# Transposed aggregations of two graphs: one 128-row matmul, or two of 64 rows into two PSUM banks

## The chip, the cores and the metric

The kernel runs on one core of a Trainium2 chip, in fp32 throughout. The metric is the device time of one execution in microseconds; before the change the median of three runs is 2634.96 us (2633.36 to 2637.23).

## The reference, cut to what matters

There are 128 graphs of 64 nodes, each node with 512 features, an adjacency matrix per graph, and four graph layers in a row. Each is followed by a residual and a layer norm: `x = layernorm(x + layer(x, adj))`. With the parts that don't matter here left out:

```python
# layer 0: attention from scores s = x @ w @ a
A = exp(leaky(8 * tanh((s_i + s_j) / 8))) * adj;  A = A / sum(A) * sum(adj)
out = A @ x @ w
# layer 1: A = adj * exp(q k^T), normalized;  out = A @ v
# layer 2: a weight per node (softmax over the graph) times x @ Wv
# layer 3: two hypergraph convolutions, G being 64 x 64 for each graph
h = layernorm(relu(G @ (x @ W1.T) + b1))          # 1024 features
out = G @ (h @ W2.T) + b2
```

In layers 0 and 3 the kernel aggregates first and multiplies by the weights after: it needs (A x)^T, (G x)^T and (G h)^T, with the features on the partitions, as the stationary operand of the product that follows.

## The kernel before, in words

Two graphs of 64 nodes make a tile of 128 rows, and two tiles (`GT = 2`) make a group, so there are 32 groups. The function `run(g)` is one group's whole way through the four layers. It is a Python generator with a `yield` between its stages; up to four groups are in flight, a new one is started every four steps, and at each step each running group emits its next stage, the newest group first. The tile framework's scheduler then orders the instructions on each engine, moves some of them past others, and puts in the semaphores. So the order within a stage of the code is not always the order on the engine, and pieces of several groups stand next to each other on TensorE.

The aggregation with transposition is `gathered(xt, bd)` (L282). For each tile `t` it takes one buffer `tr` of the pool `ps_tr` (two buffers, one PSUM bank each: 4 chunks x 128 columns of fp32), and for each of the four chunks of 128 features runs one matmul (L288):

```python
nc.tensor.matmul(tr[:, c, :], xt[:, t, ts(c, P)], bd[:, t, :], start=True, stop=True)
```

The stationary operand is the tile's x, 128 rows by 128 features. The moving operand is `bd`, a block-diagonal matrix of 128 x 128: it holds the 64 x 64 matrices of the tile's two graphs, with zeros outside the two blocks. After each tile ScalarE copies the bank to SBUF (L289). `gathered` is called in layer 0 with `e_bd` (result used by L296 with `w0_sb`) and in layer 3 with `g_bd` (used by L296 with `w3a_sb`). The second aggregation of layer 3, of `h` with its eight chunks, is written out in `run` at L502 and copied at L503 into one tile `ghT` per `t`; it feeds L296 with `w3b_sb`.

Around these on TensorE stand: `transposed` (L278), which uses the same pool `ps_tr` and is emitted twice per step, for two different groups; `product_T` (L305) and `product` (L296); `scores` (L320), which for each chunk issues two matmuls of 128 rows with 64 stationary and 64 moving columns, one per graph, into different halves of the PSUM partitions; L374, matmuls of the same kind for the layer-0 scores; `row_sums` (L327), which multiplies a block-diagonal matrix by one column of ones; L419, L440 and L458 of layers 1 to 3.

Of the other engines: VectorE does the residuals and layer norms (L346 is the last step of a norm), ScalarE the copies out of PSUM and the exponentials (L447 are those of layer 2, which wait for the maximum `mx` of VectorE), GpSimd the power for the norm and some additions, and SyncE the loads and stores.

Of the kernel before, what the change touches and what calls it, by code (L numbers as in the profile page):

```python
# [10 lines left out]
FP = mybir.dt.float32  # L11
# [4 lines left out]
P = 128  # L16
B, N, D, DH = 128, 64, 512, 1024
T = B * N // P
GT = 2
# [3 lines left out]
KC = D // P  # L23
KH = DH // P
# [7 lines left out]
def kernel(  # L32
# [23 lines left out]
    nc = tc.nc  # L56
    cpool = ctx.enter_context(tc.tile_pool(name="const", bufs=1))
    xpool = ctx.enter_context(tc.tile_pool(name="xpool", bufs=IN_FLIGHT + 1))
    chunks = ctx.enter_context(tc.tile_pool(name="chunks", bufs=3))
    scratch = ctx.enter_context(tc.tile_pool(name="scratch", bufs=1))  # L60
    stage = ctx.enter_context(tc.tile_pool(name="stage", bufs=2))
    work = ctx.enter_context(tc.tile_pool(name="work", bufs=3))
    small = ctx.enter_context(tc.tile_pool(name="small", bufs=2 * IN_FLIGHT))
    ps_mm = ctx.enter_context(tc.tile_pool(name="ps_mm", bufs=4, space=bass.MemoryType.PSUM))
    ps_tr = ctx.enter_context(tc.tile_pool(name="ps_tr", bufs=2, space=bass.MemoryType.PSUM))
# [9 lines left out]
    halves = ((slice(0, N), slice(0, N)), (slice(N, P), slice(N, P)))  # L75
# [50 lines left out]
    def weights(w, rows, cols, name, pool=None):  # L126
        t_ = (pool or cpool).tile([P, rows // P, cols], FP, name=name)
        nc.gpsimd.dma_start(out=t_, in_=w.rearrange("(c p) o -> p c o", p=P))
        return t_
# [22 lines left out]
    w3b_sb = weights(w3b, DH, D, "w3b_sb")  # L152
# [120 lines left out]
    def transposed(xt):  # L273
        xT = work.tile([P, KC, GT * P], FP, name="xT")
        for t in range(GT):
            tr = ps_tr.tile([P, KC, P], FP, name="tr")
            for c in range(KC):
                nc.tensor.transpose(tr[:, c, :], xt[:, t, ts(c, P)], ident)  # L278
            nc.scalar.copy(xT[:, :, ts(t, P)], tr)
        return xT  # L280

    def gathered(xt, bd):  # L282

        gT = work.tile([P, KC, GT * P], FP, name="xT")
        for t in range(GT):
            tr = ps_tr.tile([P, KC, P], FP, name="tr")
            for c in range(KC):
                nc.tensor.matmul(tr[:, c, :], xt[:, t, ts(c, P)], bd[:, t, :], start=True, stop=True)  # L288
            nc.scalar.copy(gT[:, :, ts(t, P)], tr)  # L289
        return gT  # L290

    def product(lhsT, t, w, cols=slice(0, D), chunks=KC):

        ps = ps_mm.tile([P, D], FP, name="mm")
        for k in range(chunks):
            nc.tensor.matmul(ps, lhsT[:, k, ts(t, P)], w[:, k, cols], start=(k == 0), stop=(k == chunks - 1))  # L296
        return ps
# [40 lines left out]
    def layer_norm(xt):  # L338
        st = small.tile([P, GT, 6], FP, name="st")
        mv = small.tile([P, GT, 2], FP, name="mv")  # L340
        for t in range(GT):
            nc.vector.bn_stats(st[:, t, :], xt[:, t, :])  # L342
            nc.vector.bn_aggr(mv[:, t, :], st[:, t, :])
        rstd = rstd_of(mv)
        for t in range(GT):
            nc.vector.tensor_scalar(xt[:, t, :], xt[:, t, :], mv[:, t, 0:1], rstd[:, t : t + 1],  # L346
                                    ALU.subtract, ALU.mult)
# [6 lines left out]
    def on_diagonal(dst, e, adj):  # L354

        for rows, cols in halves:
            nc.vector.tensor_mul(dst[rows, :, cols], e[rows], adj[rows])
        return dst


    def run(g):
        xt = xs.pop(g)
# [9 lines left out]
        for t in range(GT):  # L372
            for rows, cols in halves:
                nc.tensor.matmul(ps[rows, t, :N], s[:, t : t + 1].to_broadcast([P, N]), ident[:, cols],  # L374
                                 start=True, stop=True)
# [4 lines left out]
        nc.scalar.activation(e, e, AF.Exp, scale=8.0)  # L380
        bd = on_diagonal(next_e(), e, adj)
        yield
        gT = gathered(xt, bd)
        f = small.tile([P, GT], FP, name="f")
        nc.vector.reciprocal(f, row_sums(bd))  # L385
        nc.vector.tensor_mul(f, f, radj)
# [8 lines left out]
        xT = transposed(xt)  # L395
# [17 lines left out]
        bd = on_diagonal(next_e(), e, adj)  # L413
# [15 lines left out]
        xT = transposed(xt)  # L429
# [29 lines left out]
        gm = next_g()  # L459
# [7 lines left out]
        yield  # L467


        gT = gathered(xt, gm)  # L470

        for t in range(GT):
            c = work.tile([P, D], FP, name="junk")
# [5 lines left out]
        h = stage.tile([P, GT, DH], FP, name="h")  # L479
# [13 lines left out]
            nc.scalar.activation(h[:, t, :], h[:, t, :], AF.Identity, bias=nm[:, t : t + 1],  # L493
                                 scale=rstd[:, t : t + 1])
        yield
        ghT = []
        for t in range(GT):
            ghT.append(work.tile([P, KH, P], FP, name="ghT"))
            for i in range(KH // KC):
                tr = ps_tr.tile([P, KC, P], FP, name="tr")  # L500
                for c in range(KC):
                    nc.tensor.matmul(tr[:, c, :], h[:, t, ts(i * KC + c, P)], gm[:, t, :], start=True, stop=True)  # L502
                nc.scalar.copy(ghT[t][:, ts(i, KC), :], tr)  # L503
        yield
        for t in range(GT):
            nc.vector.tensor_add(xt[:, t, :], product(ghT[t], 0, w3b_sb, chunks=KH), xt[:, t, :])  # L506
        layer_norm(xt)
        nc.sync.dma_start(out=out_g[g], in_=xt)

# [5 lines left out]
    while g < NG or running:  # L515
        if g < NG and len(running) < IN_FLIGHT and step % APART == 0:
            running.append(run(g))
            g += 1
            if g < NG:
                load(g)  # L520
            if g % GC == 1 and g // GC + 1 < T // CT:
                load_adj(g // GC + 1)
            if g % GC == 2 and g // GC + 1 < T // CT:
                prepare_chunk(g // GC + 1)
        for r in reversed(list(running)):
            if next(r, running) is running:
                running.remove(r)
        if step == 2:
            prepare_1()
        if step == 4:  # L530
            prepare_2()
        if step == 7:
            prepare_3()
        step += 1
# [41 lines left out]
```

## Time and profile before

| | |
|---|---|
| median of 3 runs | 2634.96 us |
| profiled execution, its own time | 2635.76 us |
| its span, first to last instruction | 2634.0 us |
| TensorE busy | 2556.3 us, 97% of the span |
| VectorE busy | 1138.0 us, 43% |
| ScalarE busy | 590.6 us, 22% |
| GpSimd busy | 546.8 us, 21% |
| mean granted TensorE clock | 0.998 |
| instruction pairs (load, multiply) on TensorE | 11272 |

In the profile PE is TensorE's multiplication and PEld its loading of the stationary operand, which overlaps with it; DVE is VectorE, ACT ScalarE, POOL GpSimd, SP SyncE. A line such as `L288 PE MATMUL tr<-g_bd,x 128*128 128x128 f32 x512` names the source line, the engine, the operation, what it writes and reads by the program's names, the stationary operand's size, that of the moving one and the number of instructions. Busy time counts overlapping instructions of an engine once; the mean of one counts the whole length of each, so for matmuls, which are pipelined, busy time divided by the count is nearer to the pace.

One matmul of the program in fp32 appears as two instruction pairs; a transpose (L278) appears as one.

### The profile page before, as it was taken

To read this page: it belongs to the slowest core of one execution; us is meant where nothing else is said; L and a number is where in the kernel's file an instruction comes from. 1 tells how busy PE (TensorE), PEld (TensorE's weight loads), DVE (VectorE), ACT (ScalarE), POOL (GpSimd) and SP (SyncE) were. 2 spreads that over 40 slices of the span, in tenths; PEclk is the share of its full clock that TensorE was granted. 3 is DMA by queue.
4 is the path that set the end of the run, shared out by engine and by line. 5 is a ranking of instruction groups with operands and counts; after the bars stand their busy time and mean duration, and the time that the engine had idled before them with its cause. 6 is when DMAs were issued, how large, how long until landed. Compare 5 with 4: busy or idle time off the path is not lost.

```text
span 2634.0 us, 27593 instructions
## 1 busy us (share of the span) xinstructions
PE 2556.3 (97%) x11272; PEld 1544.1 (59%) x11272; DVE 1138.0 (43%) x2552; ACT 590.6 (22%) x1164; POOL 546.8 (21%) x560
## 2 busy tenths in 40 slices
PE   6999999999999999999999999999999999999998
PEld 4565565655565655565655565655665655665654
DVE  3535453445433455433545434445443445433443
ACT  0222221222221222221122221222221222221221
POOL 4211221212211222211312212212212212211211
PEclk9999999999999999999999999999999999999999
DMA  5000000000000000000000000000000000000000
GB/s 217 32 1 17 5 17 17 16 17 13 8 16 17 21 17 8 10 17 20 17 16 4 14 21 17 17 17 1 17 16 17 17 17 0 17 16 8 9 9 16
DMA packets 22190, 50.31 MB, mean 19 GB/s; under 512 B 1504, under 2 KB 1504, under 8 KB 22064
## 3 DMA queue, kind: packets, MB, share of 16 engines
q1 hardware_dynamic: 18560, 35.66, 4.0%
q0 software_dynamic: 3504, 12.89, 1.3%
q8 instruction: 89, 1.46, 0.2%
q14 instruction: 37, 0.30, 0.0%
HBM read 31.76 MB, written 16.78 MB: 18 GB/s over the span
## 4 chain that ended last, share of the span: by engine, by line
PE 87%; DVE 5%; issue 5%; POOL 3%; DMA 0%; ACT 0%; POOLq 0%; DVEq 0%
PE mm L296 57%; PE mm L305 17%; PE tr L288 4%; PE sm L320 2%; POOL rstd L335 2%; DVE x L346 2%; PE tr L278 1%; DVE x L420 1%; PE mm L169 1%; PE mm L225 1%; DVE x L389 1%; PE mm L419 1%; PE sm L327 1%; PE sm L374 0%; DMA junk<-in_a_dram 0%
## 5 line engine op out<-in xcount | busy, mean ns | idle before, releaser
L296 PE MATMUL mm<-wv_sb,xT 128*128 128x512 f32 x1024 | 460.6, 593 | 0.0
L305 PE MATMUL mm<-xT,m_sb 128*128 128x256 f32 x2048 | 458.3, 381 | 2.1 <-DVE hw L254 1.5
L296 PE MATMUL mm<-w3a_sb,xT 128*128 128x512 f32 x1024 | 448.0, 595 | 0.0
L296 PE MATMUL mm<-w3b_sb,ghT 128*128 128x512 f32 x1024 | 444.7, 592 | 0.0
L305 PEld LDWEIGHTS mm<-xT,m_sb 128*128 128x128 f32 x2048 | 385.7, 190 | 70.8 <-issue 17.9
L335 POOL TENSOR_TENSOR rstd<-ve,mhalf 128x2 f32<-128x2 f32 x160 | 127.7, 798 | 1369.9 <-DVE ve L333 1291.0
L296 PEld LDWEIGHTS mm<-w3b_sb,ghT 128*128 128x128 f32 x1024 | 194.5, 190 | 244.4 <-issue 244.4
L296 PEld LDWEIGHTS mm<-w3a_sb,xT 128*128 128x128 f32 x1024 | 191.9, 190 | 231.7 <-issue 229.6
L296 PEld LDWEIGHTS mm<-wv_sb,xT 128*128 128x128 f32 x1024 | 187.2, 190 | 185.8 <-issue 183.9
L385 DVE RECIPROCAL f<-sm 128x2 f32<-128x2 f32 x32 | 5.5, 171 | 617.9 <-PE sm L327 617.9
L296 PE MATMUL mm<-w_sb,xT 128*128 128x512 f32 x512 | 225.2, 593 | 0.4 <-issue 0.4
L346 DVE TENSOR_SCALAR x<-x,mv,rstd 128x512 f32<-128x512 f32 x256 | 185.3, 765 | 75.2 <-POOL rstd L335 75.2
L342 DVE BATCH_NORM_STATS2 st<-x 128x6 f32<-128x512 f32 x256 | 176.0, 688 | 4.7
L485 DVE TENSOR_TENSOR h<-mm,b3a_b 128x512 f32<-128x512 f32 x128 | 88.5, 692 | 193.4 <-PE mm L296 193.4
L296 PEld LDWEIGHTS mm<-w_sb,xT 128*128 128x128 f32 x512 | 97.0, 190 | 122.3 <-issue 122.2
L486 ACT ACTIVATE h<-h 128x512 f32<-128x512 f32 x128 | 80.6, 630 | 387.7 <-DVE h L485 387.7
L506 DVE TENSOR_TENSOR x<-mm,x 128x512 f32<-128x512 f32 x64 | 44.3, 691 | 277.0 <-PE mm L296 277.0
L476 POOL TENSOR_SCALAR x<-x 128x512 f32<-128x512 f32 x64 | 39.7, 620 | 559.9 <-PE tr L288 559.9
L502 PE MATMUL tr<-g_bd,h 128*128 128x128 f32 x1024 | 125.7, 282 | 5.5 <-ACT h L493 5.5
L487 DVE BATCH_NORM_STATS2 st<-h 128x6 f32<-128x512 f32 x128 | 88.8, 694 | 88.4 <-ACT h L486 88.4
L309 ACT ACTIVATE z<-mm,r_c 128x256 f32<-128x256 f32 x128 | 60.6, 473 | 293.7 <-PE mm L305 293.7
L502 PEld LDWEIGHTS tr<-g_bd,h 128*128 128x128 f32 x1024 | 121.3, 195 | 7.7 <-ACT h L493 7.4
(138 smaller groups left out, 2374.4 us busy)
## 6 DMA issues: line engine op xcount, KB each, us to landing
x<-in_x_dram SPq DMA_DIRECT2D x32, 512.0 KB, 3.7
out_dram<-x SPq DMA_DIRECT2D x32, 512.0 KB, 2.8
adj<-in_adjT_dram SPq DMA_DIRECT2D x8, 256.0 KB, 2.8
wv_sb<-in_wv_dram POOLq DMA_DIRECT2D x2, 1024.0 KB, 15.3
w3a_sb<-in_w3a_dram POOLq DMA_DIRECT2D x1, 2048.0 KB, 17.4
w3b_sb<-in_w3b_dram POOLq DMA_DIRECT2D x1, 2048.0 KB, 16.4
h<-in_wqk_dram POOLq DMA_DIRECT2D x2, 1024.0 KB, 5.7
w_sb<-in_w_dram POOLq DMA_DIRECT2D x1, 1024.0 KB, 10.7
```

What stands on the lines that cost most here:

```text
L288: nc.tensor.matmul(tr[:, c, :], xt[:, t, ts(c, P)], bd[:, t, :], start=True, stop=True)
L296: nc.tensor.matmul(ps, lhsT[:, k, ts(t, P)], w[:, k, cols], start=(k == 0), stop=(k == chunks - 1))
L305: nc.tensor.matmul(pz[:, : GT * P], w[:, k, ts(c, P)], xT[:, k, :], start=(k == 0), stop=(k == KC - 1))
L309: nc.scalar.activation(zT[:, c, :], pz[:, : GT * P], AF.Identity, bias=bias[:, c : c + 1])
L320: nc.tensor.matmul(ps[rows, t, :N], zT[:, k, tok], xT[:, k, tok], start=(k == 0), stop=(k == KC - 1))
L335: nc.gpsimd.tensor_tensor(rstd, ve, mhalf, ALU.pow)
L342: nc.vector.bn_stats(st[:, t, :], xt[:, t, :])
L346: nc.vector.tensor_scalar(xt[:, t, :], xt[:, t, :], mv[:, t, 0:1], rstd[:, t : t + 1], ALU.subtract, ALU.mult)
L485: nc.vector.tensor_add(hi, product(gT, t, w3a_sb, ts(i, D)), b3a_b[:, ts(i, D)])
L486: nc.scalar.activation(hi, hi, AF.Relu)
L487: nc.vector.bn_stats(st[:, t, i, :], hi)
L502: nc.tensor.matmul(tr[:, c, :], h[:, t, ts(i * KC + c, P)], gm[:, t, :], start=True, stop=True)
```

## The change

`gathered` now takes both tiles of a group at once and runs, for each chunk and tile, one matmul per graph. `halves` is the pair of slices (0 to 63, 0 to 63) and (64 to 127, 64 to 127): the stationary operand is the 64 rows of one graph by 128 features, the moving operand that graph's own 64 x 64 block of `bd`. The matmuls of the first graphs of the two tiles go into one `tr` buffer, those of the second graphs into the other, and they alternate. When both buffers are full, two ScalarE copies of 128 x 512 (8 runs of 64 columns each) sort them into the destination. The written-out loop for `ghT` is replaced by two calls of `gathered`, of four chunks each, and `ghT` becomes one tile for both `t`, in one buffer where there were three of half the size. The zeros of `bd` outside its blocks are no longer read here, but are still read by `row_sums` and L419.

```diff
-    def gathered(xt, bd):
-        gT = work.tile([P, KC, GT * P], FP, name="xT")
-        for t in range(GT):
-            tr = ps_tr.tile([P, KC, P], FP, name="tr")
-            for c in range(KC):
-                nc.tensor.matmul(tr[:, c, :], xt[:, t, ts(c, P)], bd[:, t, :], start=True, stop=True)
-            nc.scalar.copy(gT[:, :, ts(t, P)], tr)
-        return gT
+    def gathered(dst, src, chunks, bd):
+        trs = [ps_tr.tile([P, KC, GT, N], FP, name="tr") for _ in halves]
+        for c in range(KC):
+            for t in range(GT):
+                for tr, (rows, cols) in zip(trs, halves):
+                    nc.tensor.matmul(tr[:, c, t, :], src[rows, t, ts(chunks + c, P)], bd[rows, t, cols],
+                                     start=True, stop=True)
+        for h, tr in enumerate(trs):
+            nc.scalar.copy(dst.rearrange("p c (t h n) -> p h c t n", h=2, n=N)[:, h], tr)
+        return dst
...
-        ghT = []
-        for t in range(GT):
-            ghT.append(work.tile([P, KH, P], FP, name="ghT"))
-            for i in range(KH // KC):
-                tr = ps_tr.tile([P, KC, P], FP, name="tr")
-                for c in range(KC):
-                    nc.tensor.matmul(tr[:, c, :], h[:, t, ts(i * KC + c, P)], gm[:, t, :], start=True, stop=True)
-                nc.scalar.copy(ghT[t][:, ts(i, KC), :], tr)
+        ghT = work.tile([P, KH, GT * P], FP, name="ghT", bufs=1)
+        for i in range(KH // KC):
+            gathered(ghT[:, ts(i, KC), :], h, i * KC, gm)
         yield
         for t in range(GT):
-            nc.vector.tensor_add(xt[:, t, :], product(ghT[t], 0, w3b_sb, chunks=KH), xt[:, t, :])
+            nc.vector.tensor_add(xt[:, t, :], product(ghT, t, w3b_sb, chunks=KH), xt[:, t, :])
```

The other two calls become `gathered(work.tile([P, KC, GT * P], FP, name="xT"), xt, 0, bd)` in layer 0 and the same with `gm` in layer 3. In the changed file the matmul stands at L289 and the copy at L292, and the lines after them are moved by three (`product` is at L299, `scores` at L323, `row_sums` at L330).

More of the change, by code (lines that the diff above doesn't have):

```diff
@@ L382, in run @@
         yield
-        gT = gathered(xt, bd)
+        gT = gathered(work.tile([P, KC, GT * P], FP, name="xT"), xt, 0, bd)
         f = small.tile([P, GT], FP, name="f")
@@ L467, in run @@
         yield
-        gT = gathered(xt, gm)
+        gT = gathered(work.tile([P, KC, GT * P], FP, name="xT"), xt, 0, gm)
         for t in range(GT):
```

## The prediction

> **What bounds the kernel now.** I read the share of each engine first, then the chain that ended last, then TensorE's waits, then the groups of instructions with shapes kept apart, then TensorE's timeline over half a period. Page parts 1 and 4:
>
> ```profile
> PE 2556.3 (97%) x11272; PEld 1544.1 (59%) x11272; DVE 1138.0 (43%) x2552; ACT 590.6 (22%) x1164; POOL 546.8 (21%) x560
> ...
> PE 87%; DVE 5%; issue 5%; POOL 3%; DMA 0%; ACT 0%; POOLq 0%; DVEq 0%
> ```
>
> TensorE sets the time; no other engine is near half. Its waits, longest first:
>
> ```profile
> PE tr L278 <- DVE x L346: 41.6, 32, 2.5
> PE mm L179 <- DVE junk L352: 16.0, 1, 16.0
> ```
>
> One wait recurs, once in each of the 32 groups: 1.3 us at the second pair of transposes, for the normalized x. The groups the change touches and their neighbours (busy us, mean ns of one):
>
> ```profile
> L502 PE MATMUL tr<-g_bd,h 128*128 128x128 f32 x1024 | 125.7, 282 | 5.5 <-ACT h L493 5.5
> L502 PEld LDWEIGHTS tr<-g_bd,h 128*128 128x128 f32 x1024 | 121.3, 195 | 7.7 <-ACT h L493 7.4 <-issue 0.2
> L288 PE MATMUL tr<-e_bd,x 128*128 128x128 f32 x512 | 65.9, 283 | 2.1 <-issue 2.1
> L288 PE MATMUL tr<-g_bd,x 128*128 128x128 f32 x512 | 63.3, 275 | 0.0
> L320 PEld LDWEIGHTS sm<-xT,z 128*64 128x64 f32 x1024 | 32.4, 138 | 0.6
> L327 PE MATMUL sm<-ones,e_bd 128*128 128x1 f32 x256 | 32.5, 231 | 0.0
> L458 PE MATMUL sm<-bhd,h_bd 128*128 128x64 f32 x128 | 17.8, 262 | 0.0
> ```
>
> One fp32 matmul of the program is two instruction pairs here, load and multiply. The aggregations take 65.9 + 63.3 + 125.7 = 254.9 us, 9.7% of the span, at 0.124 to 0.129 us a pair. The reader is to see that L458, which streams 64 columns, costs 17.8 / 128 = 0.139 and L327, which streams one, 32.5 / 256 = 0.127: **below 128 streamed columns the time of a pair does not fall**. The loads lie end to end (121.3 of 125.7 us at L502). TensorE's timeline (start, length, count):
>
> ```profile
> 1033.60 13.90 PE L296 MATMUL mm<-w3b_sb,ghT 128*128 128x512 f32 x32
> 1047.43 0.45 PE L374 MATMUL sm<-ident,s 128*64 128x64 f32 x8
> 1047.81 7.17 PE L305 MATMUL mm<-xT,m_sb 128*128 128x256 f32 x32
> 1054.82 7.03 PE L296 MATMUL mm<-wv_sb,xT 128*128 128x512 f32 x16
> 1061.68 7.07 PE L305 MATMUL mm<-xT,m_sb 128*128 128x256 f32 x32
> 1068.59 1.95 PE L288 MATMUL tr<-g_bd,x 128*128 128x128 f32 x16
> 1070.38 2.00 PE L288 MATMUL tr<-e_bd,x 128*128 128x128 f32 x16
> 1072.21 0.50 PE L327 MATMUL sm<-ones,e_bd 128*128 128x1 f32 x4
> 1072.64 1.15 PE L320 MATMUL sm<-xT,z 128*64 128x64 f32 x32
> 1073.62 1.10 PE L320 MATMUL sm<-z,xT 128*64 128x64 f32 x32
> ```
>
> From start to start, L288 takes (1070.38 - 1068.59) / 16 = 0.112 us a pair. L320, whose two graphs write different halves of the columns, takes (1073.62 - 1072.64) / 32 = 0.031 us, though its 64-column load lasts 138 ns: two parts of the array work side by side.
>
> [...] 192 ns against 138 for 64 columns fewer is 54 ns, and 0.112 us is such a load. That halving the rows saves nothing no run here shows yet. [...] row tiles (64 x 128) do not occur before. [...] L296 before it runs 0.431 a pair, so it would have handed over at 1033.60 + 32 x 0.431 = 47.38, not 47.43; L374's four side-by-side steps of 0.058 (0.98 us over L320's 16 steps, less entry) are 0.23, not 0.38; the L305 block after it takes 7.01 us against 6.91 for the same block at 1061.68. In and out: 0.05 + 0.15 + 0.10 = **0.30 us**. [...]
>
> **The change part by part**, for one of 32 groups; the order is that which the scheduler gives the changed program.
>
> 1. *Streaming.* Per chunk and tile, two pairs of 128 rows become four of 64 rows with half the columns. Each still loads 128 columns, 0.112 us. If the two row tiles run side by side: 2 x 0.112, as before, so **zero** on 32 matmuls. Bounds: a load of half the rows at half the time would save 16 x 0.056 = 0.9 us in each of four blocks; loads taking turns would cost 16 x 0.112 = 1.8. I take zero, by L320's side-by-side loads.
> 2. *Mode changes.* Four new row-tile blocks: the g aggregation after L288's place, the e aggregation, two for ghT, none next to each other. I take 0.35 each, L374's 0.30 and 0.05 for a first load of 128 instead of 64 columns (54 ns); half to double as bounds. g's block is split in two in 6 groups: 0.35 x 38 / 32 = 0.42. The e block now stands in the middle of L320's first block (7 matmuls before, 9 behind), and a way out and in of that mode was there already: 0.30. ghT: 0.70. Sum **1.4 us**.
> 3. *Order within e.* In 29 groups the e block starts with four matmuls of one bank, then four of the other: the second bank is not yet copied out. Four steps of 2 x 0.112 have no partner: **+0.9**, bounds 0 (a tile overlapping its own two passes) and 0.9. The second ghT block starts two and two: +0.2.
> 4. *Waits for the banks.* Both buffers of tr are now filled by one call and freed by its two ScalarE copies (588 ns each, unchanged in size). The copy starts 0.33 us after the last multiply starts (1069.68 for the eighth L288 at 1068.59 + 7 x 0.112), so the banks are free at 0.9 and 1.5. Between g and e lie four L327 pairs, 14 L320 pairs and mode changes, 0.45 + 0.43 + 0.3 = 1.2; between the ghT calls one L296 matmul, 0.86 and a mode change, 1.15; the second bank is first touched 0.45 (ghT) or 0.9 (e) later. **Zero**, up to 0.5 each if a copy is late. ScalarE now has L447's exponentials between the two ghT pairs; they wait for VectorE's mx, and before, they ran from 1023.9; the second ghT block ends about 1024.3, so they are done in time.
> 5. *The wait of L278.* Before the second x's transposes the changed order has three single L296 matmuls and all four other tr blocks, where there was one. From the start of ghT: 0.35 + 1.8 + 0.86 + 0.35 + 2.0 + 0.86 + 0.9 + 0.86 = 8.0 us, against 7.5 before with a wait of 1.9 in it:
>
> ```profile
> 1019.08 3.84 PE L502 MATMUL tr<-g_bd,h 128*128 128x128 f32 x32
> ...
> 1026.57 0.63 PE L278 MATMUL tr<-ident,x 128*128 128x128 f32 x4 [1.92 <-DVE x L346]
> ```
>
> VectorE's queue keeps its order, so x is there, in this group by 0.5 us and by more in those with shorter waits: **-1.3**; the L296 matmuls are only moved. What is late next: nothing on TensorE in this stretch.
> 6. *Other queues.* SP's DMAs, POOL's and VectorE's work are the same and in the same order; the L320 scores finish about 3 us later, but their result is wanted at L419, 24 us on. ghT in one buffer is rewritten 79 us later, 50 after its last read. Zero; without that cover a delay of 3 us in the scores would reach TensorE. The last group has no L296 to lie under its banks: +2 us once.
>
> Sum per group: 1.4 + 1.1 - 1.3 = +1.2; 32 x 1.2 + 2 = **+41 us** on the profiled execution's 2635.8 (span 2634.0 and 1.8 around it), 2677. The median of the runs lies 0.8 below that execution: **2676**.
>
> **The rivals.**
> *A, the case above*: side by side, 128-column loads set the pace. Its own range, with steps 2 and 3 at their bounds, 2641 to 2740. For it: L320, L327 and L458. 68%.
> *B, faster*: the wait at L278 goes, and what is added is under 1.3 us a group, from which point it decides. Mode changes at half (0.7), e's order free, ghT's 0.2: 0.9 - 1.3 = -0.4, 32 x -0.4 + 2 = -11: 2624. Loads at half the time, a stronger form, would take off 3.6 us more a group. For it: the lone wait is surely reached later. Against: L374 and L320 both show the full price. 12%.
> *C, far slower*: the two row tiles take turns at one load path, unlike column tiles. Three blocks at +1.8, e's remaining four steps +0.9, less the 0.2: +6.1 a group, 2676 + 195 = 2871. For it: no row tiles in this trace. [...] 14%.
> *D, nothing to see*: A with e's order free and cheaper changes, +0.2 a group or less: about 2636. 6%. That the kernel doesn't do what it says I exclude: its matmuls are of 64 columns and alternate between two tr buffers.
>
> **How the numbers follow.** A change of under 0.2% can't be told from none here. Faster 0.12 (B), same 0.06 (D), slower 0.82 (A and C). The time is A's, 2676. The range leaves out C and B's stronger form: 2620 to 2740.
>
> **What would show it.** Right: twice as many aggregation pairs (4096) with about the same busy time, 0.06 us a pair; L278's wait for x near zero; blocks of L288's place of 1.8 us with gaps of 0.1 to 0.2 about them; the first half of e at twice the pace per matmul. Wrong: a busy time of the aggregations near 450 us (C), or near 130 us (loads at half); a new wait of TensorE for ScalarE's copies of over 0.5 us a group; L278's wait still there.

## The result, and the profile after

The changed kernel takes 2664.43 us (median of 4 runs, 2663.2 to 2668.45) beside 2634.16 for the kernel before: a ratio of 1.0116, 95% interval 1.0099 to 1.0134, or 30 us slower. The forecast was 2676 with a range of 2620 to 2740. First the page, parts 1 and 4, then TensorE's waits (us in total, times, longest):

```profile
span 2663.9 us, 31654 instructions
...
PE 2621.5 (98%) x13320; PEld 1585.2 (60%) x13320; DVE 1097.3 (41%) x2552; ACT 580.4 (22%) x1164; POOL 543.5 (20%) x560
...
PE 97%; issue 1%; DVE 1%; DMA 0%; POOL 0%; ACT 0%; POOLq 0%; DVEq 0%
```

```profile
PE mm L179 <- DVE junk L355: 15.6, 1, 15.6
PE tr L278 <- DVE x L349: 4.2, 2, 2.5
```

TensorE is busy for 65 us more and sits idle for 35 us less. The wait at L278 fell from 41.6 us in 32 places to 4.2 in two. The chain that ended last is now TensorE almost throughout. The aggregations, with shapes kept apart, and one line of their loads:

```profile
L289 PE MATMUL tr<-g_bd,h 64*128 64x64 f32 x2048 | 138.6, 280 | 6.7 <-ACT h L496 6.0 <-ACT ghT L292 0.7
L289 PE MATMUL tr<-e_bd,x 64*128 64x64 f32 x1024 | 82.3, 285 | 1.8 <-issue 1.8
L289 PE MATMUL tr<-g_bd,x 64*128 64x64 f32 x1024 | 66.6, 276 | 0.0
L289 PEld LDWEIGHTS tr<-g_bd,h 64*128 64x128 f32 x2048 | 129.2, 192 | 36.4 <-ACT ghT L292 24.4 <-ACT h L496 9.3 <-ACT e L450 0.8
```

The number of pairs doubled to 4096; their busy time went from 254.9 to 287.5 us, 0.07 a pair, though the loads, now of 64 rows, still take 187 to 195 ns on average by group, where those of 128 rows took 192 to 195. In g's block the multiplies start two and two, 7 ns apart, with 0.111 us from one two to the next. So the row tiles do run side by side, and that only makes good the doubled number of loads. TensorE's timeline over a group (start, length, count) shows where the rest goes:

```profile
1027.70 0.56 PE L461 MATMUL sm<-bhd,h_bd 128*128 128x64 f32 x4
1028.19 2.00 PE L289 MATMUL tr<-g_bd,h 64*128 64x64 f32 x32
1030.12 1.12 PE L299 MATMUL mm<-wv_sb,xT 128*128 128x512 f32 x2
1031.18 2.17 PE L289 MATMUL tr<-g_bd,h 64*128 64x64 f32 x32
...
1041.14 13.90 PE L299 MATMUL mm<-w3b_sb,ghT 128*128 128x512 f32 x32
...
1069.22 7.07 PE L308 MATMUL mm<-xT,m_sb 128*128 128x256 f32 x32
1076.22 2.00 PE L289 MATMUL tr<-g_bd,x 64*128 64x64 f32 x32
1078.15 0.61 PE L330 MATMUL sm<-ones,e_bd 128*128 128x1 f32 x4
1078.69 0.68 PE L323 MATMUL sm<-xT,z 128*64 128x64 f32 x14
1079.30 2.50 PE L289 MATMUL tr<-e_bd,x 64*128 64x64 f32 x32
1081.72 0.74 PE L323 MATMUL sm<-xT,z 128*64 128x64 f32 x17
...
1083.38 14.00 PE L299 MATMUL mm<-w3a_sb,xT 128*128 128x512 f32 x32
```

From its start to the next line's, g's block takes 1.93 us where L288's took 1.79. e's takes 2.42 and stands within the scores. From L461 to the product with w3b it is 1041.14 - 1027.70 = 13.44 us, with no wait in it.

What L278's wait was made of shows on VectorE and GpSimd. First the kernel before, then the changed one, in the group after the one above:

```profile
1103.16 2.68 POOL L402 TENSOR_TENSOR x<-x,bv_b 128x512 f32<-128x512 f32 x2
1103.23 2.89 DVE L346 TENSOR_SCALAR x<-x,mv,rstd 128x512 f32<-128x512 f32 x2 [0.58 <-POOL rstd L335]
1104.85 0.63 PE L278 MATMUL tr<-ident,x 128*128 128x128 f32 x4 [1.14 <-DVE x L346]
```

```profile
1111.95 1.00 DVE L349 TENSOR_SCALAR x<-x,mv,rstd 128x512 f32<-128x512 f32 x2 [0.57 <-POOL rstd L338]
1113.00 1.04 PE L278 MATMUL tr<-ident,x 128*128 128x128 f32 x8
1113.69 3.27 POOL L405 TENSOR_TENSOR x<-x,bv_b 128x512 f32<-128x512 f32 x2 [1.77 <-PE tr L278]
1114.74 1.04 PE L278 MATMUL tr<-ident,x 128*128 128x128 f32 x8
```

Before, the two norm steps that the transposes wait for ran beside GpSimd's addition on the other group's x, and took 2.89 us; now they are done before that addition starts, and take 1.00. The addition itself waits for the first transposes, and these stand later in the new order. Over the whole trace, 58 of the 256 norm steps lay for over 80% of their length beside such an addition before, at 1.48 us on average against 0.54 for the 191 with no GpSimd work beside them; in the changed kernel it is one, at 1.48. So of the 1.14 us that TensorE waited here, by estimate 0.9 (1.48 - 0.54, for the first of the two norm steps) come from the longer norm. In this group the later place of the transposes would by itself have hidden even that: they now start 1114.74 - 1111.95 = 2.79 us after the norm does.

### The profile page after: what moved, and what is told of

Same layout as the page of the kernel before. It is cut to its first block, busy times and chain, and to the rows that moved or that the text cites. A ratio compares the mean times of both kernels' runs of the same rounds, so it can differ in the third digit from the quotient of the medians.

```text
span 2663.9 us, 31654 instructions
## 1 busy us (share of the span) xinstructions
PE 2621.5 (98%) x13320; PEld 1585.2 (60%) x13320; DVE 1097.3 (41%) x2552; ACT 580.4 (22%) x1164; POOL 543.5 (20%) x560
## 4 chain that ended last, share of the span: by engine, by line
PE 97%; issue 1%; DVE 1%; DMA 0%; POOL 0%; ACT 0%; POOLq 0%; DVEq 0%
PE mm L299 58%; PE mm L308 17%; PE tr L289 10%; PE sm L323 3%; PE mm L422 2%; PE tr L278 2%; PE sm L330 1%; PE mm L169 1%; PE mm L225 1%; PE sm L461 0%; PE sm L377 0%; DMA junk<-in_a_dram 0%; PE sm L443 0%; PE sm L188 0%; DVE junk L355 0%
## 5 line engine op out<-in xcount | busy, mean ns | idle before, releaser
L299 PE MATMUL mm<-wv_sb,xT 128*128 128x512 f32 x1024 | 473.4, 600 | 0.0
L308 PE MATMUL mm<-xT,m_sb 128*128 128x256 f32 x2048 | 458.3, 381 | 2.1 <-DVE hw L254 1.5
L299 PE MATMUL mm<-w3a_sb,xT 128*128 128x512 f32 x1024 | 448.4, 596 | 1.2 <-ACT xT L292 1.2
L299 PE MATMUL mm<-w3b_sb,ghT 128*128 128x512 f32 x1024 | 447.2, 595 | 0.0
L308 PEld LDWEIGHTS mm<-xT,m_sb 128*128 128x128 f32 x2048 | 385.7, 190 | 70.7 <-issue 17.9
L299 PEld LDWEIGHTS mm<-w3b_sb,ghT 128*128 128x128 f32 x1024 | 195.3, 191 | 245.5 <-issue 245.4
L299 PEld LDWEIGHTS mm<-w3a_sb,xT 128*128 128x128 f32 x1024 | 192.2, 190 | 233.3 <-issue 229.7
L299 PEld LDWEIGHTS mm<-wv_sb,xT 128*128 128x128 f32 x1024 | 184.9, 190 | 175.4 <-issue 169.2
L299 PE MATMUL mm<-w_sb,xT 128*128 128x512 f32 x512 | 225.2, 593 | 0.9 <-issue 0.9
L299 PEld LDWEIGHTS mm<-w_sb,xT 128*128 128x128 f32 x512 | 97.0, 190 | 122.8 <-issue 115.8
L349 DVE TENSOR_SCALAR x<-x,mv,rstd 128x512 f32<-128x512 f32 x256 | 132.0, 558 | 75.5 <-POOL rstd L338 75.4
L289 PEld LDWEIGHTS tr<-g_bd,h 64*128 64x128 f32 x2048 | 129.2, 192 | 36.4 <-ACT ghT L292 24.4
L289 PE MATMUL tr<-g_bd,h 64*128 64x64 f32 x2048 | 138.6, 280 | 6.7 <-ACT h L496 6.0
```

The source lines that it names most:

```text
L289: nc.tensor.matmul(tr[:, c, t, :], src[rows, t, ts(chunks + c, P)], bd[rows, t, cols], start=True, stop=True)
L308: nc.tensor.matmul(pz[:, : GT * P], w[:, k, ts(c, P)], xT[:, k, :], start=(k == 0), stop=(k == KC - 1))
```

## The experiments

**One part of the change alone.** Two kernels: the first splits only ghT by rows, the second only g and e.

```diff
 # e1: gathered as before; the new function under another name, for ghT alone
+            gathered_halves(ghT[:, ts(i, KC), :], h, i * KC, gm)
...
 # e2: the new gathered for g and e; ghT as before
+                    nc.tensor.matmul(tr[:, c, :], h[:, t, ts(i * KC + c, P)], gm[:, t, :], start=True, stop=True)
```

> Only the ghT aggregation of layer 3 is split by rows; the g and e aggregations are as before. My theory: the split itself costs two blocks with a change of tiling mode and a start of two and two (about +0.9 us a group), and the order that comes with it removes the wait at L278 (-1.3 us a group). By the two traces the terms of this part are: ghT pairs +14.7 us, the L296 pieces next to them +8 to +11, L458 +2.7, L278 -43.2. So 2634 - 15 = about 2619, faster than before. Rival, that row tiles cost wherever they stand and the wait at L278 is not what pays: over 2634, about 2650 (half of the +30).

> Only the g and e aggregations are split by rows; ghT is as before. My theory: all of the cost and none of the gain: e +19.4 us, g +7.6, the scores around e +11.3, L327 +3.3, L305 +3.5, and the wait at L278 stays at about 42: 2634 + 45 = about 2679, slower than the full change. Rival, that the cost is spread evenly over the blocks: about 2650.

Measured: ghT alone 2618.9 us, ratio 0.9942 (0.9928 to 0.9955); g and e alone 2680.66, ratio 1.0172 (1.0158 to 1.0186). The change is a gain of 15 us and a loss of 46 put together. TensorE's waits, in the first and in the second:

```profile
PE tr L278 <- DVE x L359: 4.4, 3, 2.5
```

```profile
PE tr L278 <- DVE x L349: 41.5, 32, 2.5
```

So the wait goes with the ghT part, and stays where only g and e are split. The norm goes with it: its 256 steps take 132.0 us in the first kernel, 558 ns on average, and in the second still 185.4, 766 ns on average.

**The order without the row tiles, and half the columns.** Is the gain of the ghT part due to its row tiles? The third kernel fills both banks in one call and copies them at its end, as the change does, but with 128-row matmuls. The fourth (e4) is the same but leaves out the second graph of each tile: it streams half the columns, and the copies put the first graph's result in both places.

```diff
 # e3
-        trs = [ps_tr.tile([P, KC, GT, N], FP, name="tr") for _ in halves]
+        trs = [ps_tr.tile([P, KC, P], FP, name="tr") for _ in range(GT)]
...
+                nc.tensor.matmul(trs[t][:, c, :], src[:, t, ts(chunks + c, P)], bd[:, t, :], start=True, stop=True)
...
+        for t, tr in enumerate(trs):
+            nc.scalar.copy(dst[:, :, ts(t, P)], tr)
 # e4, against e3
+                nc.tensor.matmul(trs[t][:, c, :N], src[:, t, ts(chunks + c, P)], bd[:, t, :N], start=True, stop=True)
...
```

> The change without its row tiles: one call fills both banks, alternating, and two copies empty them at the end, but each matmul is of 128 rows, one bank per tile. My theory: the wait at L278 goes with the order alone (-42 us), e in the middle of the scores costs a mode change (+10): about 2604, faster than both. Rival, that the wait goes because the row-tile blocks take longer: the wait stays for most of its length, 2630 to 2645.

> As the kernel with both banks and 128-row matmuls, but each aggregation streams only the 64 columns of the tile's first graph (the second graph's are left out and the first's are copied twice). My theory, that the 128-column load sets the pace: the same time as with 128 columns within 5 us, 0.112 us a pair still. Rival, that streamed columns count: [...]

Measured: 2607.09 us, ratio 0.9896 (0.9882 to 0.9909), and with half the columns 2603.12, ratio 0.9882 (0.9869 to 0.9896). The third kernel's wait at L278, its g block with shapes kept apart, and then that of the fourth:

```profile
PE tr L278 <- DVE x L347: 4.4, 3, 2.5
...
L288 PE MATMUL tr<-g_bd,x 128*128 128x128 f32 x512 | 63.3, 275 | 0.0
L288 PEld LDWEIGHTS tr<-g_bd,x 128*128 128x128 f32 x512 | 63.1, 192 | 2.4 <-issue 0.5
```

```profile
L288 PE MATMUL tr<-g_bd,x 128*128 128x64 f32 x512 | 61.3, 271 | 0.0
L288 PEld LDWEIGHTS tr<-g_bd,x 128*128 128x128 f32 x512 | 63.1, 192 | 2.4 <-issue 0.5
```

The loads' 63.1 us is the same to the digit, and half the columns take 2 us off g's 63.3, and 4 us off the whole kernel. Streaming as the limit would by estimate have taken 110: 1024 x 2 pairs at 0.054, an eighth of the 0.431 us that a pair of L296 takes for 512 columns. Two things follow. The wait at L278 goes with the order of instructions, not with the rows of a tile: it is 4.4 us here with 128 rows. And a block takes the time of its 128-column loads, 63.1 of 63.3 us for g. Beside the third kernel, which has its order, the changed kernel takes 57 us more: that is what the row tiles cost.

**The place of e.** In the fifth kernel here (e6), the changed kernel takes e's two banks from `ps_mm`, so that e needn't wait for g's copies; the sixth (e7) does the same to the kernel with 128-row matmuls.

```diff
-        trs = [ps_tr.tile([P, KC, GT, N], FP, name="tr") for _ in halves]
+        trs = [(pool or ps_tr).tile([P, KC, GT, N], FP, name=name) for _ in halves]
...
-        gT = gathered(work.tile([P, KC, GT * P], FP, name="xT"), xt, 0, bd)
+        gT = gathered(work.tile([P, KC, GT * P], FP, name="xT"), xt, 0, bd, ps_mm, "mm")
```

> The changed kernel with the e aggregation's two banks taken from the pool ps_mm instead of ps_tr, so that it needn't wait for g's copies, alternates throughout and follows g directly. My theory: e's four steps without partner (0.5 us a group) and a mode change in the middle of the scores (0.3) go: 2664 - 26 = about 2638. Rival, that the two held banks of ps_mm keep the products of w3a waiting: 2664 or more, with a new wait at L299.

> 128-row matmuls filling both banks per call, with e's banks from ps_mm so that it follows g and the scores stay whole. My theory: one mode change of about 0.3 us a group less than with e in the middle of the scores: 2607 - 10 = about 2597, the fastest. Rival: held banks of ps_mm make L297 wait: 2607 or more.

Measured: 2635.11 us, ratio 1.0002 (0.9994 to 1.0011), and 2592.69, ratio 0.9841 (0.9828 to 0.9855). The timeline of the first of the two, with row tiles:

```profile
1058.87 7.07 PE L308 MATMUL mm<-xT,m_sb 128*128 128x256 f32 x32
1065.87 2.00 PE L289 MATMUL tr<-g_bd,x 64*128 64x64 f32 x32
1067.70 1.95 PE L289 MATMUL mm<-e_bd,x 64*128 64x64 f32 x32
1069.59 0.60 PE L330 MATMUL sm<-ones,e_bd 128*128 128x1 f32 x4
1070.12 1.15 PE L323 MATMUL sm<-xT,z 128*64 128x64 f32 x32
```

And of the second, with 128 rows:

```profile
1044.25 7.07 PE L306 MATMUL mm<-xT,m_sb 128*128 128x256 f32 x32
1051.15 1.95 PE L288 MATMUL tr<-g_bd,x 128*128 128x128 f32 x16
1052.94 1.95 PE L288 MATMUL mm<-e_bd,x 128*128 128x128 f32 x16
1054.73 0.50 PE L328 MATMUL sm<-ones,e_bd 128*128 128x1 f32 x4
1055.16 1.15 PE L321 MATMUL sm<-xT,z 128*64 128x64 f32 x32
```

Alternating from its start and next to g, e costs 1.89 us instead of 2.42. From the start of L308 or L306 to the scores it is 11.25 us with row tiles and 10.91 without: 0.34 more. By this comparison that is the price of entering and leaving the row-tile blocks, which the prediction and the expectations call a mode change; the traces show the time and not what the engine does in it. Both kernels' products of w3a start on time; the rival's wait for `ps_mm` didn't come. The sixth kernel is the fastest here: all of the change's gain in order, and no row tiles. With that order the row tiles still cost 42 us (2635.11 against 2592.69).

**Neighbours on one row tile.** Three kernels change only the order within a call. Below, a pass is one of the two instruction pairs of an fp32 matmul, and a step is the 0.112 us from one start to the next that L288 takes with its 128-column loads; two passes of different row tiles share a step in the changed kernel's g block, where they start 7 ns apart.

```diff
 # e5: AAAAAAAABBBBBBBB
+        for tr, (rows, cols) in zip(trs, halves):
+            for c in range(KC):
+                for t in range(GT):
...
 # e8: AABB, four times
+        for c in range(KC):
+            for tr, (rows, cols) in zip(trs, halves):
+                for t in range(GT):
 # e9: AAAABBBBAAAABBBB
+        for cc in range(0, KC, 2):
+            for tr, (rows, cols) in zip(trs, halves):
+                for c, t in ((cc, 0), (cc, 1), (cc + 1, 0), (cc + 1, 1)):
```

> The changed kernel with the loops turned: all eight matmuls of the first graphs, then all eight of the second, so neighbours are on the same row tile. If row tiles run side by side only when their instructions alternate, and strictly in order, each block takes 32 steps of 0.112 us instead of 16: four blocks x 32 groups x 1.8 = +229 us, less the 16 which the order within e costs already, about 2870. If, as the trace of the changed kernel hints (the second bank's first multiply started at the fifth of the first bank's eight), the second half may run up to four steps ahead: 28 steps, +172, about 2810. If row tiles never ran side by side: 2664, no change.

> The changed kernel with the order AABB in place of ABAB: two matmuls (four passes) of one row tile, then two of the other. My theory, read off the turned loops: a multiply of the other row tile may start while up to four passes ahead of it are still to come, so four passes in a row are wholly hidden: 2664, within 5 us of the changed kernel, and blocks of 1.9 us. Rival, that only neighbouring instructions run side by side: at least half the steps lose their partner, +8 steps x 0.112 us x 3 blocks x 32 groups = +86, about 2750.

> The changed kernel with the order AAAABBBBAAAABBBB: eight passes of one row tile at a time. My theory: four of each eight passes are hidden, so a block takes 20 steps of 0.112 us instead of 16: +0.45 us in g's and the two ghT blocks, e's about as before (21 steps already): 2664 + 43 = about 2707, if the clock holds. Rival, that row tiles without a partner also bring the clock down, as with the turned loops (granted clock 0.916 there): over 2720 and a granted clock under 0.98.

Measured: 2987.62 us for eight in a row, ratio 1.1337 (1.132 to 1.1355), above all three expectations; 2679.83 for two in a row, 1.0179 (1.0157 to 1.02), 16 us over the changed kernel and so past its 5; 2782.17 for four in a row, 1.0555 (1.0536 to 1.0574), where the rival was right. What the first two missed is the clock. Four stretches of the first of the three (length; busy time of PE, PEld, DVE, ACT and POOL with the number of instructions; granted clock; DMA share; GB/s):

```profile
1201.00:1204.00 3.00, 3.00 (x30) 2.73 (x28) 0.00 (x0) 0.96 (x2) 0.00 (x0) 1.00 0.02 5
1204.00:1207.80 3.80, 3.80 (x38) 3.70 (x37) 0.00 (x0) 0.59 (x1) 3.26 (x4) 0.88 0.00 0
1207.80:1212.00 4.20, 4.20 (x65) 4.17 (x66) 0.33 (x2) 1.17 (x4) 0.39 (x1) 0.50 0.00 0
...
1240.00:1244.00 4.00, 4.00 (x29) 4.00 (x27) 1.99 (x8) 1.17 (x2) 1.13 (x1) 0.62 0.00 0
```

In the middle of the kernel the granted clock goes to 0.50 within two such blocks in a row, most of whose steps hold one pass alone. By estimate, with each stretch ending at half clock, that is 5.6 us after the start of g's block at 1201.28 (0.88 over 3.80 us) and 4.4 us after that of ghT's at 1236.58 (0.62 over 4.00 us). TensorE is busy for the whole of each stretch, and the scores that follow the first two blocks run at 0.50. Over the run the clock is 0.916. By estimate (1 - 0.916) x 2988 = 251 us are lost to it, against (1 - 0.993) x 2664 = 19 in the changed kernel. That leaves 324 - 232 = 92 us for the order. The steps show that the notion of four passes was right and its sum was not:

```profile
1201.28 3.06 PE L289 MATMUL tr<-g_bd,x 64*128 64x64 f32 x29
1204.06 0.32 PE L289 MATMUL tr<-e_bd,x 64*128 64x64 f32 x1
1204.17 0.27 PE L289 MATMUL tr<-g_bd,x 64*128 64x64 f32 x1
1204.22 0.27 PE L289 MATMUL tr<-e_bd,x 64*128 64x64 f32 x1
...
1204.39 0.27 PE L289 MATMUL tr<-g_bd,x 64*128 64x64 f32 x1
1204.45 3.44 PE L289 MATMUL tr<-e_bd,x 64*128 64x64 f32 x29
```

e's first multiply starts while three of g's are still to start, although all of g's stand before it in the program, and the two then take turns. The scheduler's order of whole matmuls can't be the reason, since 29 passes are fourteen and a half matmuls. The same happens between the halves of one call, and now also between calls that follow each other: two calls take 16 + 3 x 12 = 52 steps, 104 a group, where the changed kernel's four blocks take about 69 (16, 16, 17 and 20). Worked out after the result, 35 x 0.112 x 32 = 125 us; e next to g and the two ghT calls next to each other save two mode changes (2 x 0.34 x 32 = 22), and e out of the scores about 0.4 x 32 = 13: 90 us.

In the other two kernels g's block takes 1.98 us (two in a row) and 2.53 (four), start to start, beside 1.93: four passes are hidden, of eight in a row about half. Their profiled clocks are 0.989 and 0.969, so (1 - 0.989) x 2673 - 19 = 10 us and (1 - 0.969) x 2780 - 19 = 67 us go to the clock.

## Why the prediction was right

*Bound and mechanism.* The forecast was that the side-by-side row tiles gain nothing since the loads of 128 columns set the pace, that mode changes and e's order cost, and that the wait at L278 gives part of it back. All three are shown: the kernel with half the columns has the same loads and nearly the same time, the splits of the change give +46 and -15, and the wait goes from 41.6 to 4.2 us. The lines that the forecast leaned on for the first, L458 and L327, did not show it by themselves: busy time over count takes in the end of each block of four, and from start to start L458's four pairs take 1019.08 - 1018.69 us, 0.098 each.

*Step 1*, zero: right. *Step 2*, mode changes at 0.35: 0.34 measured on g with e. *Step 4*, no waits for banks: right in the steady part; TensorE's waits have 1.9 us of them in all (0.7 at L289, 1.2 at L299), at the end. *Step 5*: right in its result, by the scheduler's order, which the third kernel has without a row tile. But it took the time at which x is ready as given, and step 6 called VectorE's and GpSimd's work unchanged; VectorE's busy time fell from 1138.0 to 1097.3 us, that of the norm step (L346, now L349) from 185.3 to 132.0. No run parts this from the later place of the transposes.

*The sum* was mis-sized in its terms. From stages of the two timelines, a group (two starts of before, not shown so far, first):

```profile
1018.69 0.56 PE L458 MATMUL sm<-bhd,h_bd 128*128 128x64 f32 x4
...
1074.66 14.00 PE L296 MATMUL mm<-w3a_sb,xT 128*128 128x512 f32 x32
```

- g with its neighbours: before 6.91 + 1.79 + 0.43, after 7.00 + 1.93 + 0.54: +0.34; forecast 0.42.
- e and the scores, from L330's end to w3a: before 3.85 (1.83 and 2.02), after 4.69: +0.84; forecast 0.30 + 0.9. The step that failed is 3: of eight passes that stand without partner in the program four were hidden, as the other row tile's passes start from the fifth on, so that e's order costs about 0.5 (2.42 - 1.93).
- ghT to w3b: 14.91 before, with a wait of 1.92 where the mean is 1.3, so 14.29; 13.44 after: -0.85; forecast 0.70 + 0.2 - 1.3 = -0.4. The row-tile blocks and their neighbours cost 0.74 where 0.9 was forecast; the transposes, now eight in a row in place of four, and the products between them take 0.3 less, which the forecast had at nothing.

Sum +0.33 instead of +1.2, or 11 us instead of 39. Against that the ends and the clock cost more than the 2 us allowed. The starts of the 32 blocks of w3b's products show where: the changed kernel is 2.4 us later at the first, loses 17.6 over the next 28, about 6 of them at half clock, and 9.9 from there to its end. By the trace's record the clock is at half for 39.7 us of the span, where it was 12.0 before, which by estimate is 14 us of time; 22.7 of the 39.7 lie in the last 40 us, where there are no other groups' matmuls and TensorE also waits. Two of the last lines of ghT:

```profile
2630.91 3.25 PE L289 MATMUL tr<-g_bd,h 64*128 64x64 f32 x28 [0.44 <-ACT h L496]
2634.83 5.01 PE L289 MATMUL tr<-g_bd,h 64*128 64x64 f32 x32 [0.67 <-ACT ghT L292]
```

The last one takes 5.01 us, at a granted clock of 0.50, for what takes 2.17 in the middle of the kernel. So it is partly luck that 2676 came within 12 us: the terms of a group were 28 us too high, the ends and the clock 17 too low, and the two errors partly cancel. The upper end of the range also doesn't come out of steps 2 and 3 as it says: at their bounds they give 2.8 + 1.1 - 1.3 = 2.6 a group, about 2720 and not 2740.

*The rivals.* C, loads taking turns, against which the trace of before had only L320's side-by-side column tiles (0.031 us a pair), is refuted by the aggregations' 287 us against the 450 that it needed. B came true for the ghT part alone, as its own point of decision said: what that part adds is less than the wait. D is excluded by the interval, whose lower end is 1.0099.

*What the forecast assumed.* That row tiles would run side by side was its estimate, from the column tiles of L320; the 0.07 us a pair now shows it. That a change of mode takes time it had from L374 alone, 0.30 us; 0.34 was measured on g with e. That half the rows don't shorten a load, which no run showed when the prediction was made, now has its number: 187 to 195 ns for 64 rows, 192 to 195 for 128. Two row tiles on one bank were not tried.

## What to carry to other kernels

Before splitting a matmul into row tiles, see whether streaming or the load takes the time. Here, at 128 stationary columns and 128 or 64 moving ones in fp32, it is the load (with half the columns g's block took 61.3 us instead of 63.3), and a load of half the rows is as long (187 to 195 ns against 192 to 195), so the split gains nothing; whether it pays where streaming takes the time, no run here shows. Look for what a rewrite does to the order around it before crediting the arithmetic: here nearly all the gain was a wait (41.6 us before, 4.4 after) that a different order of the same matmuls removed, and that order without row tiles, with e's banks from another pool, gives 2592.69 us, 1.6% below the kernel before. When TensorE waits for another engine, look also at what runs beside that engine's work: by estimate most of this wait was a norm step that took longer beside GpSimd's addition (1.48 us against 0.54). Whether holding back that addition alone would have removed it was not tried. If row tiles are used, put their blocks next to each other, and alternate them matmul by matmul: with e next to g and alternating the kernel took 2635.11 us instead of 2664.43. Two in a row nearly kept g's block at its time (1.98 us beside 1.93), but the kernel lost 16 us and its clock, 0.992 to 0.994 when alternating, was 0.982 to 0.989.

## What the runs showed of the hardware that was not expected

- A multiply of the other row tile starts ahead of up to three passes that stand before it in the program, and beside a fourth: in the kernel with eight in a row e's first starts at 1204.06, after the 29th of g's 32; in the e block of the changed kernel the second bank's first starts 6 ns after the fifth of the first bank's eight.
- A busy TensorE can lose its clock: in the kernel with eight in a row the granted clock was 0.50 over 4.20 us, all of them busy. It fell with the length of the stretches on a single row tile. Over all executions it was 0.996 to 0.999 without row tiles, 0.995 to 0.996 with all blocks alternating (e6), 0.992 to 0.994 in the changed kernel, whose e starts with four in a row, 0.982 to 0.989 with two in a row throughout, 0.968 to 0.972 with four and 0.916 to 0.918 with eight. What exactly is measured to grant it no run here separates.
- A norm step of VectorE (128x512) took 0.54 us on average with no GpSimd work beside it and 1.48 beside GpSimd's addition of 128x512, in the kernel before. That it is the addition that stretches it is read from these averages; no run changed it alone.
